# A metaformer block on one core: interleaved channel pairs and small pieces in the scan, and the norm's inverse root as a power on POOL

## The chip, the cores and the metric

The kernel runs on one core of a Trainium2 chip, in fp32 throughout. The metric is the device time of one execution in microseconds (us). PE is TensorE (matmul), DVE is VectorE, ACT is ScalarE, POOL is GpSimd, and SP is SyncE, which issues nearly all of the kernel's DMAs.

## The reference, cut to what matters

The input is 8 samples of 384 channels and 32 x 32 positions. Each sample is read as L = 1024 tokens of C = 384 channels. The layer adds a state-space ("mamba") branch with an MLP, then a feed-forward branch with sign-binarised weights and activations that are quantised by sample:

```python
t = (t - mu) * rsqrt(var + 1e-05) * ln_w + ln_b       # after a norm over channels, eps 1e-6
xm, z = split(t @ in_proj_w.T)                        # 768 channels each
xc = silu(conv3(xm) + conv_b)                         # causal, three taps
dt, Bm, Cm = split(xc @ x_proj_w.T, [24, 24 + 16])
dt = softplus(dt @ dt_proj_w.T + dt_proj_b)
dA = exp(dt[..., None] * -exp(A_log));  dBu = (dt * xc)[..., None] * Bm[:, :, None, :]
h = dA_t * h + dBu_t;  y_t = sum_n(h * C_t)           # a scan over 1024 tokens, 16 states
y = (y + xc * D) * silu(z)
x = x + gelu((y @ out_proj_w.T) @ mlp_w1.T + b1) @ mlp_w2.T + b2
t = t + ffn(norm(t))     # two "bitlinear" layers with gelu between; samples 0 to 4 only
```

The bitlinear layers quantise in five groups along the batch of 8, so that a group is one sample and the samples 5 to 7 get zero from the feed-forward branch.

## The kernel before, in words

**Who sets the order.** The kernel first writes down all operations as a list (`write_down`, `Plan.add`), each with an engine, a planner's cost in us, what it reads and writes (whole tiles or parts of them), and a priority, called lane. `Plan.run` then goes through a planned time, picks for each engine what can start, and emits the instructions in that order. Each engine runs its own instructions strictly in that order on the chip; the plan's times play no part any more. Lane 0 is the scan, 1 and 4 the front of the coming samples (`s1` and its norms), 2 the back (`s3`), 5 and 6 the feed-forward part, 7 the binarising of weights, and -1 the scan's sums on PE. On DVE and POOL the planner prefers ready work of lanes above 0. Small evictions of PSUM and affine steps (`affine`) may go to ACT or to DVE (or POOL), whichever is free. Costs come from formulas such as `c_act`, `c_dve` and `c_pool`. Where PE would idle in the plan for over 0.7 us, a `spare` matmul (L412) is put in that has no use but to occupy PE. Tiles come from rings of a fixed number of buffers (`self.rings`); an operation that needs a new buffer waits until one is free. PSUM has three buffers for matmul results (`mm`), one for the scan's sums (`y`), and two of double size for `da`.

**The front, `s1`.** For each sample and each half of 512 tokens: `norm` (L543) makes the mean by matmuls with ones (`p_sum`), spreads it over the partitions by a matmul (`p_mean`, L567), subtracts on DVE (L578), squares on ACT, sums again (`p_var`), takes Sqrt on ACT on 128x128 (with a table load where the table was another), the reciprocal on DVE (L590), spreads this (`p_r`), and multiplies on DVE (L592). Then come `p_in` and the convolution (L661), Silu over all six channel blocks at once (one 128x3072 instruction), `p_dbc` (the x_proj), `p_bc` (which adds the two halves of B and C, L703), six `p_dt` matmuls (L722) with 24 useful rows each, Softplus over 128x3072, six products dt * xc on POOL (L732), the stores of xc, z, dt and dtx to DRAM as whole tiles of 128x3072, and `p_z` with Silu.

**The scan, `s2`, `scan`, `scan_tile`.** A unit is 64 channels with 16 states over 1024 tokens (in samples 0 and 7: 128 channels over 512), so 12 units a sample. It is handled in tiles of 128 partitions = 32 channels x 4 states: two tiles for each of four quads of states, eight in a unit. For each tile: ACT makes exp(dt * A) into `da` (L510), POOL multiplies `u = dtx_r * B` (L886), DVE scans (L890; the result goes to `u` or `da`), and the product with C is made on POOL (L904) or DVE (L907), as `on_pool` says by quad and unit. PE adds the four states and folds into `py` with four matmuls of 32 columns side by side (L842), for two quads together. `dt_r` and `dtx_r` are copies of rows from DRAM, each repeated on four partitions.

**The back, `s3` and `ffn`.** `s3` has `p_out` (36 matmuls a sample), `p_h` and `p_o` (72 each) with Gelu on half of the hidden channels at once (128x3072). `ffn` has two `p_y` layers for samples 0 to 4, clipping on POOL (L1088) and Gelu on 128x3072. `binarise` sums the weights' columns by matmuls with ones (L1018), once.

Of the kernel before, what the change touches and what calls it, by code (L numbers as in the profile page):

```python
# [33 lines left out]
P = 128  # L34
B, C, L = 8, 384, 1024
KC = C // P
DI = 768
# [5 lines left out]
HK = KH // 2  # L43
T = 512
# [49 lines left out]

def c_pool(n):
    return 0.18 + n * 0.00214
# [33 lines left out]
class Piece:  # L130
# [8 lines left out]

    def __getitem__(self, part):  # L140
        return self, part

# [209 lines left out]
class Layer:  # L352
    def __init__(self, ctx, tc, a, out):
# [9 lines left out]
        def ring(tag, bufs, where=sbuf):  # L363
# [7 lines left out]
            "front": ring("front", 2), "t_f": ring("t_f", 2), "w_f": ring("w_f", 3),  # L371
            "dbc": ring("dbc", 1), "halo": ring("halo", 2),

            "dt_r": ring("dt_r", 3), "dtx_r": ring("dtx_r", 3), "u": ring("u", 9),
# [4 lines left out]
            "yg": ring("yg", 1), "hid": ring("hid", 2), "t_b": ring("t_b", 1), "w_b": ring("w_b", 3),  # L379
            "w6": ring("w6", 2), "w6_n": ring("w6_n", 2), "res": ring("res", 2),  # L380

            "t_n": ring("t_n", 2), "small": ring("small", 7),

            "mm": ring("mm", 3, psum), "sq": ring("sq", 1),
            "rstd": ring("rstd", 2),
# [6 lines left out]
        for b in range(B):  # L392
            for name in ("dt", "dtx"):
                self.dram[name, b] = handed(f"{name}_d{b}", [DI, L])
# [24 lines left out]

    def constants(self):
        nc, a, const = self.nc, self.a, self.const
        small = const.tile([P, 3], F32, name="small")
        one, self.eps_m, self.eps_f = (small[:, i : i + 1] for i in range(3))
        for at, value in ((one, 1.0), (self.eps_m, E1 * E2), (self.eps_f, E_FFN)):
            nc.vector.memset(at, value)
# [8 lines left out]
        self.pick = const.tile([P, 2 * NS], F32, name="pick")  # L436
        nc.vector.tensor_add(self.pick, ident[:, DQ : 2 * DQ], ident[:, DP + DQ : DP + 2 * DQ])
        self.edge = const.tile([P, KD, 2], F32, name="edge")
# [50 lines left out]
    def matmuls(self, p, w, t, k0, n, start, stop, r, claim, w0=0):  # L489


        def emit():
            for k in range(n):
                self.nc.tensor.matmul(  # L494
                    p.real, w.real[:, w0 + k, :], t.real[:, k0 + k, :],
                    start=start and k == 0, stop=stop and k == n - 1,
                )
# [45 lines left out]
    def norm(self, t, eps, scale):  # L543
# [17 lines left out]
        def spread(src, name):  # L561
            p = self.piece("mm", [P, T], name)

            def emit():
                for g in range(G):
                    one = self.ident[:, g * DQ : g * DQ + 1].to_broadcast([P, P])
                    nc.tensor.matmul(  # L567
                        p.real[:, g * TG : (g + 1) * TG], one, src.real, start=True, stop=True
# [16 lines left out]
        rstd = self.piece("rstd", [P, TG], "rstd")  # L585
        self.act(
            lambda: rstd.real, lambda: p_var.real, AF.Sqrt, c_act(TG), r=[p_var], w=[rstd],
# [684 lines left out]
```

## Time and profile before

| | |
|---|---|
| three runs | 3261.88 us median (3261.76 to 3268.25) |
| the profiled execution, device time | 3262.23 us |
| its span, first to last instruction | 3260.4 us, granted TensorE clock 0.984 |
| ACT table loads | 222 x 1283 ns, 284.8 us |
| exp into `da`, 128x1024 | 576 x 1116 ns, 639.4 us |
| scans on DVE, 128x1024 | 312 x 2285 ns and 264 x 2278 ns |
| `p_h`, `p_o` matmuls on PE | 513.6 and 506.7 us |
| DMA | 748.73 MB, mean 230 GB/s, 68.5% of 16 engines |

One matmul of 128x512 in fp32 is two records on PE, of 592 ns each and overlapping. A row of a group gives line, engine, operation, output and inputs, shape, count, then busy time, mean ns of one, and the idle time of the engine just before with what ended most of it. Busy time is the union of the records, so that it can be less than count times mean. "L494" and "L510" are helpers that emit most matmuls and activations; there the tile's name tells them apart.

### The profile page before, as it was taken

What the parts mean: (1) busy time and instruction counts of PE and PEld (TensorE: products, weight loads), DVE (VectorE), ACT (ScalarE), POOL (GpSimd) and SP (SyncE); (2) the same over time, 40 slices, a digit from 0 to 9 for tenths busy, and PEclk for the clock granted to TensorE, in tenths of its full rate; (3) what the DMA queues carried; (4) which work ended last, traced back from release to release, by engine and by line L of the source; (5) the groups of instructions that cost most, each with busy time, mean ns of one, the idle gap of its engine ahead of it and who ended that gap; (6) DMA issues with size and microseconds to landing.
All of it is one profiled execution on the core that took longest, in us unless ns stands there. A gap on an engine that the chain in (4) does not pass through costs nothing.

```text
span 3260.4 us, 34027 instructions
## 1 busy us (share of the span) xinstructions
PE 3122.5 (96%) x11098; PEld 1317.7 (40%) x11098; DVE 2742.3 (84%) x2127; ACT 2024.3 (62%) x2246; POOL 2848.7 (87%) x1371
## 2 busy tenths in 40 slices
PE   8988999999999999999899999999999999999999
PEld 4333433444433434334334344343443534433334
DVE  4778899799978899888998878999788988789880
ACT  4778787656665576665656566755666565656551
POOL 1688899979999989999989999989999899999970
PEclk9998999999999999999999999999999999999999
DMA  6988778657796568675686667866677656766542
GB/s 218 305 282 276 249 250 294 221 183 234 259 322 197 184 230 291 229 238 197 208 298 211 237 211 246 295 225 226 220 275 250 207 185 205 249 187 207 167 141 76
DMA packets 367345, 748.73 MB, mean 230 GB/s; under 512 B 33856, under 2 KB 111168, under 8 KB 367168
## 3 DMA queue, kind: packets, MB, share of 16 engines
q1 hardware_dynamic: 366736, 746.46, 68.5%
q8 instruction: 89, 1.46, 0.2%
q14 instruction: 88, 0.72, 0.1%
q10 hardware_dynamic: 432, 0.09, 0.0%
HBM read 566.06 MB, written 180.36 MB: 229 GB/s over the span
## 4 chain that ended last, share of the span: by engine, by line
PE 74%; DMA 9%; DVE 6%; ACT 5%; issue 2%; POOL 2%; SPq 1%; ACTq 0%; DVEq 0%; POOLq 0%
PE p_y L494 17%; PE p_o L494 14%; PE p_h L494 13%; PE py L842 9%; PE p_out L494 6%; PE p_z L494 6%; PE p_in L494 5%; DVE da L890 2%; DMA w<-in_out_proj_w 2%; DMA w_f<-in_in_proj_w 2%; DVE u L890 1%; ACT L510 1%; DMA w_b<-in_mlp_w 1%; ACT da L510 1%; PE spare L412 1%
## 5 line engine op out<-in xcount | busy, mean ns | idle before, releaser
L886 POOL TENSOR_TENSOR u<-dtx_r,bc 128x1024 f32<-128x1024 f32 x768 | 1790.4, 2362 | 72.3 <-DMA dtx_r<-dtx_d 46.3
L510 ACT ACTIVATE da<-dt_r,a_neg 128x1024 f32<-128x1024 f32 (+1 forms) x960 | 902.7, 945 | 534.0 <-DVE u L907 331.1
L904 POOL TENSOR_TENSOR u<-u,bc 128x1024 f32<-128x1024 f32 x352 | 828.4, 2364 | 121.5 <-DVE u L890 115.5
L890 DVE TENSOR_TENSOR_SCAN da<-da,u 128x1024 f32<-128x1024 f32 (+1 forms) x416 | 840.5, 2020 | 111.6 <-POOL u L886 62.9
L890 DVE TENSOR_TENSOR_SCAN u<-da,u 128x1024 f32<-128x1024 f32 (+1 forms) x352 | 699.5, 2010 | 90.3 <-ACT da L510 63.0
L494 PE MATMUL p_h<-t,w_b 128*128 128x512 f32 x1152 | 513.6, 600 | 10.9 <-DMA w_b<-in_mlp_w 9.9
L907 DVE TENSOR_TENSOR u<-da,bc 128x1024 f32<-128x1024 f32 x416 | 507.9, 1221 | 10.5 <-ACT state L901 0.3
L494 PE MATMUL p_o<-g,w 128*128 128x512 f32 x1152 | 506.7, 595 | 5.4 <-ACT g L510 2.9
L842 PE MATMUL py<-u,fold 128*32 128x512 f32 x3072 | 376.6, 605 | 4.5 <-DVE u L907 4.5
L494 PEld LDWEIGHTS p_h<-t,w_b 128*128 128x128 f32 x1152 | 214.7, 190 | 298.1 <-issue 256.4
L494 PEld LDWEIGHTS p_o<-g,w 128*128 128x128 f32 x1152 | 215.9, 190 | 292.0 <-issue 277.3
L494 PE MATMUL p_y<-tn,w_b 128*128 128x512 f32 x720 | 324.9, 598 | 4.0 <-DVE tn L592 3.3
L494 PE MATMUL p_y<-gf,w_n 128*128 128x512 f32 x720 | 319.0, 599 | 6.7 <-DMA w_n<-bin_w 4.0
L510 ACT ACT_TABLE_LOAD x222 | 284.8, 1283 | 11.7 <-DVE xc L661 7.3
L494 PE MATMUL p_out<-yg,w 128*128 128x512 f32 x552 | 249.2, 604 | 8.9 <-DMA w<-in_out_proj_w 4.3
L494 PE MATMUL p_z<-t,w_f 128*128 128x512 f32 x504 | 232.5, 611 | 8.2 <-DMA w_f<-in_in_proj_w 6.2
L494 PE MATMUL p_in<-t,w_f 128*128 128x512 f32 x504 | 228.3, 602 | 10.8 <-DMA w_f<-in_in_proj_w 8.6
L494 PEld LDWEIGHTS p_y<-gf,w_n 128*128 128x128 f32 x720 | 135.1, 191 | 187.6 <-issue 172.4
L494 PEld LDWEIGHTS p_y<-tn,w_b 128*128 128x128 f32 x720 | 133.9, 190 | 183.9 <-issue 155.4
L842 PEld LDWEIGHTS py<-u,fold 128*32 128x32 f32 x3072 | 81.5, 110 | 261.1 <-issue 203.2
L525 ACT ACTIVATE g<-p_h,v_vecs 128x512 f32<-128x512 f32 x157 | 106.3, 681 | 120.9 <-PE p_h L494 120.7
L525 ACT ACTIVATE y<-p_y,v_vecs 128x512 f32<-128x512 f32 x138 | 94.1, 683 | 130.0 <-PE p_y L494 100.3
(112 smaller groups left out, 2700.3 us busy)
## 6 DMA issues: line engine op xcount, KB each, us to landing
dtx_r<-dtx_d SPq DMA_DIRECT2D x144, 512.0 KB, 5.8
dt_r<-dt_d SPq DMA_DIRECT2D x144, 512.0 KB, 6.0
w_b<-in_mlp_w SPq DMA_DIRECT2D x192, 192.0 KB, 2.9
w<-in_mlp_w SPq DMA_DIRECT2D x96, 384.0 KB, 3.6
w_f<-in_in_proj_w SPq DMA_DIRECT2D x168, 192.0 KB, 4.2
y_d<-y SPq DMA_DIRECT2D x120, 256.0 KB, 3.4
gf<-y_d SPq DMA_DIRECT2D x20, 1536.0 KB, 9.5
xc_d<-xc SPq DMA_DIRECT2D x16, 1536.0 KB, 7.3
```

The lines of the kernel that those rows point to most:

```text
L412: self.plan.fill = lambda: self.nc.tensor.matmul(self.plan.spare.real[:, : 2 * P], self.ones, self.one.to_broadcast([P, 2 * P]), start=Tru ...
L494: self.nc.tensor.matmul(p.real, w.real[:, w0 + k, :], t.real[:, k0 + k, :], start=start and k == 0, stop=stop and k == n - 1,)
L510: lambda: self.nc.scalar.activation(out(), in_(), func, **{k: v() if callable(v) else v for k, v in kw.items()}),
L525: nc.scalar.activation(out(), in_(), AF.Identity, bias=bias, scale=scale)
L842: nc.tensor.matmul(py.real[p0 : p0 + DQ, :], self.fold, hc, start=False, stop=(q == NQUAD - 1), skip_group_check=True,)
L886: add("POOL", 2.36, lambda: nc.gpsimd.tensor_mul(u.real, dtx_r.real, spread(bq)), r=[dtx_r, bq], w=[u])
L890: add("DVE", (0.2 if half else 0.15) + n * 0.00209, lambda k=k, col=col: nc.vector.tensor_tensor_scan(to.real[:, k, :], da.real[:, k, :], ...
L904: add("POOL", 2.36, lambda: nc.gpsimd.tensor_mul(u.real, u.real, spread(cq)), r=[cq], w=[u])
L907: add("DVE", 1.21, lambda: nc.vector.tensor_mul(u.real, da.real, spread(cq)), r=[da, cq], w=[u])
```

## The change

It has several parts at once.

1. **Interleaved pairs.** dt * xc is stored with two channel blocks' values side by side: `[.., n, 2]`. `scan_tile` becomes `scan_pair`, which handles two tiles: one POOL product over 128x2048 (two of 128x1024 in samples 0 and 7) with the B or C row repeated for each pair of neighbours, two scans and, on DVE, two products that read or write every second element. The product of the last quad is made in place in `dtx_r`. `on_pool` puts the second products of quads 0 and 2, and of quad 1 in every fourth unit, on POOL.
2. **Rings.** `u` has 3 buffers (of double size) in place of 9, `dtx_r` 2 (double) in place of 3.
3. **Small pieces.** Tiles of 128x3072 (`xc`, `z`, `dt`, `yg`, `g`, `gf`) become three or six pieces of 128x1024 with buffers of their own; activations, clips, loads and stores go piece by piece. `mlp_out` issues its matmuls by two.
4. **The norm.** The variance is scaled and evicted (ACT or DVE), turned by a matmul so that it stands in four columns, gets eps added on DVE, and is raised to -0.5 on POOL over 128x4. Sqrt and the reciprocal go.
5. **dt_proj and the rows.** One matmul (`p_all`) adds the halves for dt, B and C and lays dt's low part on two groups of 32 rows; two dt matmuls of 32 rows each then go as a pair. The B and C rows are stored by one DMA instead of four.
6. **Binarising.** The column sums use 32 columns of PE for each of three or four blocks, and the group sums are made by DVE reductions and one more matmul.

The diff's core (layouts of the weights on the host follow the new order of channels and are left out):

```diff
+def c_pair(n):
+    return 0.19 + n * 0.00188
...
-            "front": ring("front", 2), "t_f": ring("t_f", 2), "w_f": ring("w_f", 3),
+            "front": ring("front", 7), "t_f": ring("t_f", 2), "w_f": ring("w_f", 3),
...
-            "dt_r": ring("dt_r", 3), "dtx_r": ring("dtx_r", 3), "u": ring("u", 9),
+            "dt_r": ring("dt_r", 3), "dtx_r": ring("dtx_r", 2), "u": ring("u", 3),
...
-            "yg": ring("yg", 1), "hid": ring("hid", 2), ... "res": ring("res", 2),
+            "yg": ring("yg", 3), "hid": ring("hid", 6), ... "res": ring("res", 4),
...
-        rstd = self.piece("rstd", [P, TG], "rstd")
-        self.act(
-            lambda: rstd.real, lambda: p_var.real, AF.Sqrt, c_act(TG), r=[p_var], w=[rstd],
-            table="sqrt", bias=eps, scale=scale,
-        )
-        add("DVE", 0.93, lambda: nc.vector.reciprocal(rstd.real, rstd.real), w=[rstd])
-        p_r = spread(rstd, "p_r")
+        var = self.piece("rstd", [P, TG], "var")
+        self.affine(lambda: var.real, lambda: p_var.real, [p_var], [var], scale=scale, n=TG)
+        p_turned = self.piece("mm", [P, G], "p_turned")
+        add("PE", 0.5, lambda: nc.tensor.matmul(
+            p_turned.real, var.real, self.ident[:, ::DQ], start=True, stop=True
+        ), r=[var], w=[p_turned])
+        rstd = self.piece("root", [P, G], "rstd")
+        add("DVE", 0.1, lambda: nc.vector.tensor_scalar_add(rstd.real, p_turned.real, eps),
+            r=[p_turned], w=[rstd])
+        add("POOL", 0.8, lambda: nc.gpsimd.tensor_tensor(
+            rstd.real, rstd.real, self.power.to_broadcast([P, G]), ALU.pow
+        ), w=[rstd])
+        p_r = spread(rstd, "p_r", True)
...
+                def two(k=k, pds=pds, dbc=dbc, ws=ws):
+                    for i in range(2):
+                        rows = slice(i * DQ, (i + 1) * DQ)
+                        nc.tensor.matmul(
+                            pds[i].real, ws[i].real[rows, (k + i) % KC, :], dbc.real[rows, :],
+                            start=True, stop=True,
+                        )
...
+                add("POOL", 2.35, lambda p=p, dtx=dtx, xc=xc, dt=dt: nc.gpsimd.tensor_mul(
+                    dtx.real.rearrange("p n i -> p i n"), xc.pieces[p].real, dt.pieces[p].real
+                ), r=[xc[2 * p], xc[2 * p + 1], dt[2 * p], dt[2 * p + 1]], w=[dtx])
...
-        return q == 0 or (q == 2 and (i == 0 or m % 3))
+        return q % 2 == 0 or (q == 1 and m % 4 == 0)
...
+        def product(t, x, row):
+            nc.gpsimd.tensor_mul(
+                u.real[:, x], t.real[:, x], row.real.unsqueeze(2).to_broadcast([P, n, 2])
             )
...
+        for x in range(wide):
+            add("POOL", c_pair(2 * n), lambda x=x: product(dtxs, x, bq), r=[dtxs[x], bq],
+                w=parts[x])
+        for t, mine in enumerate(cols):
+            da = self.piece("da", [P, wide, n], "da")
+            dt_r = dts[t]
...
+            def in_u(i, t=t):
+                return u.real[:, 0, :, t] if wide == 1 else u.real[:, t, :, i]
...
+                        nc.vector.tensor_mul(u.real[:, 0, :, t], da.real[:, 0, :], cq.real)
...
+        if on_pool:
+            for x in range(wide):
+                add("POOL", c_pair(2 * n), lambda x=x: product(u, x, cq), r=[cq], w=parts[x])
```

The sums then read every second element, `u.real[:, 0, h, i]`, where `u` is viewed as `[P, wide, n, 2]` with the halves of the tokens as `h`:

```diff
-                        for p0, hc in parts:
+                        parts = [u.real[:, 0, h, i] for i in both for h in HALVES] if (
+                            half is None) else [u.real[:, x, :, i] for i in both for x in both]
+                        for g, hc in enumerate(parts):
                             nc.tensor.matmul(
-                                py.real[p0 : p0 + DQ, :], self.fold, hc,
+                                py.real[g * DQ : (g + 1) * DQ, :], self.fold, hc,
```

## The prediction, as put on record

> **What bounds the kernel now.** I read the page's busy shares first, then the same shares over three stretches (up to the first scan product on POOL at 105 us, from there to the last scan sum on PE at 3178 us, and the tail), then the groups and who waits for whom.
>
> ```profile
> PE 3122.5 (96%) x11098; PEld 1317.7 (40%) x11098; DVE 2742.3 (84%) x2127; ACT 2024.3 (62%) x2246; POOL 2848.7 (87%) x1371
> ```
> ```profile
> 0.00:105.00 105.00, 90.77 (x444) 46.50 (x446) 43.04 (x61) 51.89 (x63) 12.67 (x18) 0.97 0.74 245
> 105.00:3178.00 3073.00, 2953.28 (x10470) 1236.72 (x10472) 2695.59 (x2062) 1956.25 (x2166) 2836.08 (x1353) 0.98 0.70 233
> 3178.00:3260.00 82.00, 78.50 (x190) 34.49 (x182) 3.70 (x5) 16.12 (x17) 0.00 (x0) 1.00 0.25 77
> ```
> ```profile
> L886 POOL TENSOR_TENSOR u<-dtx_r,bc 128x1024 f32<-128x1024 f32 x768 | 1790.4, 2362 | 72.3 <-DMA dtx_r<-dtx_d 46.3
> L904 POOL TENSOR_TENSOR u<-u,bc 128x1024 f32<-128x1024 f32 x352 | 828.4, 2364 | 121.5 <-DVE u L890 115.5
> L907 DVE TENSOR_TENSOR u<-da,bc 128x1024 f32<-128x1024 f32 x416 | 507.9, 1221 | 10.5 <-ACT state L901 0.3
> L842 PE MATMUL py<-u,fold 128*32 128x512 f32 x3072 | 376.6, 605 | 4.5 <-DVE u L907 4.5
> ```
> ```profile
> L722 PE MATMUL p_dt<-dbc,w_f 128*128 128x512 f32 x168 | 81.9, 620 | 9.5 <-ACT dt L525 6.0 <-ACT rows L523 3.4
> L722 PE MATMUL p_dt<-dbc,w_b 128*128 128x512 f32 x24 | 11.4, 608 | 0.9 <-DVE xc L661 0.9
> L412 PE MATMUL spare<-small 128*128 128x256 f32 x314 | 80.0, 396 | 0.1
> L590 DVE RECIPROCAL rstd<-rstd 128x128 f32<-128x128 f32 x26 | 24.2, 937 | 1.8 <-ACT rstd L510 1.3
> ```
> ```profile
> PE p_r L567 <- DVE rstd L590: 10.5, 6, 3.7
> ```
>
> The reader is to see that no engine bounds it alone. (The rows of the second fence give, for each stretch, its length, then busy us and count of PE, PEld, DVE, ACT and POOL, then clock, DMA share and GB/s; the groups give count, busy us, mean ns of one, and the idle time before them with its cause.) In the scan stretch of 3073 us PE is busy 2953 (96%), but about 71 of that is the `spare` filler, which the planner puts only where PE would have nothing: useful PE work is 2882, so PE lacks work for 191 us. POOL is busy 92%, DVE 88%. The 96 units (8 samples, 12 each) take 32.0 us each; of these PE needs 30.0, POOL 29.5, DVE 28.1. Three nearly equal loads that hand work to each other lose 2 us per unit in waiting: POOL waits 115.5 us for DVE's scans, and PE runs into filler. A saving on one engine pays only if the others leave room. The tail is PE alone.
>
> [...] The interleaved tiles are read every 8 bytes[...]; no row of before shows such a stride. [...] four `py` matmuls take 376.6/384 = 0.98 us.
>
> **The change, part by part.** Counts after the change are from the order of the built programs.
>
> *POOL products.* Removed: 1790.4 + 828.4 us. Added: 450 of 2048 elements and 304 of 1024 (754 where there were 1120, though DVE's share of the second products falls from 416/768 to 332/768). The new shape, one operand repeated for each two neighbours, is in no row of before, so its price is bounded. Above: nothing is gained, two of today's less one fixed part,[...] 4.50 us. Below: one-input rows on POOL take 0.93 ns per element (2898 ns at 3072, 1474 at 1536), two-input ones 2.12 (2362 at 1024, 1275 at 512); if the repeated operand is read half as often, half of the difference goes, 1.53 ns, 3.3 us. The middle is 3.9. I take 4.04 (2.12 at 1024): near the middle, and the value that the diff's c_pair gives the planner, whose c_pool, c_act and c_dve lie within 1.1% of the rows that the trace does show (2.371 against 2.362, 1.110 against 1.116, 1.234 against 1.221). An estimate, then. 450 x 4.04 + 304 x 2.12 = 2462 against 2619: -157. At 4.50 (2.36): +124; at 3.3 (1.75): -602.
> *Other POOL.* `dtx` 48 x 2.36 = 113 for 118.6; clipping in 60 pieces of 1.0 (from 2.898 at 3072 and 1.474 at 1536 elements) 60 for 57.9; edge and state copies 104 x 0.2 = 21 for 15; the power of 4 elements 26 x 0.8 = 21 (0.2 as the smallest POOL rows, to 2: 5 to 52). Together +23. POOL: -134, to about 2715; at 4.50 +147; at 3.3 -579.
> *DVE.* 84 fewer products x 1.221 = -103; 26 reciprocals -24; 26 additions x 0.155 = +4; binarising's reductions replace others of about their size. -123. Strided scans I take at today's 2.28[...]; 0 to +100 if not.
> *ACT.* 48 fewer table loads x 1.283 = -62, Sqrt -9 and +6 for its affine, 300 pieces x 1.116 instead of 278 = +57, wider copies +4: about -4. At 62% this is off the path: if its cover went, a whole 57 us would show.
> *PE.* p_dt: 96 matmuls, 93.3 us, become 48 pairs. Side by side 0.97 each (46.6), else 93; I take 1.07: -42. p_all 16 x 0.97 instead of p_bc's 6.7: +9. p_turned 26 x 0.3 = +8. The binarising sums, 18.7, in six sets at `py`'s 0.98: -13. Net -38 (to +4 without overlap).
> *Waits.* The norm's root now goes PE, DVE, POOL, PE. Behind POOL's queue it waits for up to one product, half of one on average (2.0); 0.27 + 0.3 + 0.16 + 0.8 + 2.0 = 3.5 us where Sqrt and reciprocal took 1.3 (2.6 with a table load). Queued behind p_r on PE is everything, since PE keeps its order; in the order after, p_r sometimes follows p_turned with only one or two small groups between. 1 to 2.2 us x 26 = 26 to 57; PE work covers most, I count 10 (0 to 50). POOL's pow also holds back at most 0.8 us of products.
> *DMAs.* SP issues 2091 before and 2255 after, at about half a us each (525 ns for `dtx_r`): 82 us more on a queue with much room; bytes of `dtx_r` are the same. Stores and loads in pieces can start earlier: small gain, counted at nothing (it is covered by PE's other work; if not, the 46.3 us that POOL waits for `dtx_r` can return, since that ring now has two buffers for one per unit).
> *Rings.* Three `u` of double size, and the last product in place of `dtx_r`: a unit's buffers come free at its two sums. With POOL leading by one pair that suffices; counted at nothing, at worst the 21.6 us POOL now waits for `py` doubles.
>
> **The sum.** Against the profiled execution (span 3260.4, device time 3262.2; the runs' median is 3261.9, so no shift). Upper case, *waiting stays*: only PE's work shrinks and the norm's wait comes on top, 3262 - 38 + 10 = 3234. Lower case, *POOL keeps its share*: (2836 - 134)/0.923 = 2927, + 105 + 82 + 2 = 3116 (the 2 is device time over span); PE's 2844 useful us in it would be 97%, which is possible, as the best slices of today reach 99%. Room on POOL and DVE is now 5 to 10% below PE's need in place of 2 to 6%, so part of the waiting must go; I have no row that gives the part and take the middle: (3234 + 3116)/2 = 3175. At 3.3 us POOL would leave PE alone as the bound: its 2844 at the 99% of its best slices is 2873, + 187 + 2 + 10 = 3072 with nothing else in the way; I put the low end at 3095, since PE's stalls on DMA and norms stay. Next late is PE's own work, then the chain scan to product to sum.
>
> **Rivals.**
> 1. *Waiting stays* because pairs double the grain: a second product waits for two scans (4.6 us). For it: the 115.5 us wait on DVE. Against: DVE gets freer too. 3234, faster still.
> 2. *The product isn't cheaper* (slower): place L886/L904's successor, price 4.50. POOL then has 2836 + 147 = 2983 in the stretch; at a share of 95% (between today's 92 and the 97 of its fullest stretches) 3140 + 189 = 3329. It decides where POOL's total is back at today's: 4.04 + 0.46 x 134/281 = 4.26 us.[...] Against: the planner's record.
> 3. *PE reads interleaved sums slowly* (slower): at double, 384 x 0.86 = +330: 3500. It decides from (3262 - 3175)/384 = 0.23 us per set.[...]
> 4. *No measurable change*: coarser waits and norm stalls eat some 90 us: 3262.
>
> **How the numbers follow.** Forecast (3095 to 3210) 0.60; rival 1 (3210 to 3255) 0.15; rival 4 within 0.2% (about what a measurement of this kernel can tell from no change) 0.05; rival 2 0.14; rival 3 and the like 0.06. Faster 0.75, same 0.05, slower 0.20. The range, 3095 to 3290, takes the forecast, rivals 1 and 4 and rival 2's milder part. The forecast's own range is 3095 to 3210.
>
> **What would show it.** The 2048-element POOL row near 4.04; POOL near 2715 and DVE near 2620 busy; p_dt under 55 us; `py` still near 377; spare filler and PE's idle time both smaller; table loads 174; p_r's wait on POOL under 25. A product above 4.26, `py` rows above 0.7 us or PE waiting long for rstd would make it wrong.

## The result, and the profile after

The changed kernel takes 3309.31 us (median of 4 runs, 3296.7 to 3317.63) against 3264.64 us for the kernel before in the same series: ratio 1.0127, 95% interval 1.0105 to 1.015. It is slower by 1.3%, where 3175 us was forecast. The profiled execution took 3317.63 us with a span of 3315.7 us and a granted clock of 0.974; before it was 3260.4 us and 0.984. So the profile explains a difference of 55 us, some ten more than the medians.

The busy shares of the page after, and the same three stretches as before (up to the first scan product on POOL, now at 95 us; up to the last scan sum, now at 3243 us; the tail):

```profile
PE 3129.7 (94%) x10964; PEld 1290.3 (39%) x10964; DVE 2643.6 (80%) x2080; ACT 1979.2 (60%) x2362; POOL 2749.3 (83%) x1050
```
```profile
0.00:95.00 95.00, 83.56 (x446) 41.84 (x446) 39.22 (x72) 47.52 (x59) 12.87 (x19) 1.00 0.70 229
95.00:3243.00 3148.00, 2977.04 (x10359) 1218.03 (x10358) 2600.88 (x2004) 1915.29 (x2283) 2736.39 (x1031) 0.97 0.70 230
3243.00:3316.00 73.00, 69.06 (x162) 30.40 (x160) 3.53 (x5) 16.38 (x21) 0.00 (x0) 1.00 0.26 78
```

The reader is to see that POOL and DVE each got about 99 us less to do (2848.7 and 2742.3 before), and that the scan stretch became 75 us longer all the same: POOL fills 87% of it, where it filled 92%. PE's busy time did not fall. The groups of the scan and of the parts that PE was to save:

```profile
L924 POOL TENSOR_TENSOR u<-dtx_r,bc 128x2048 f32<-128x2048 f32 x216 | 881.6, 4093 | 162.3 <-PE py L889 111.0 <-issue 45.9 <-POOL dtx_r L924 3.3
L924 POOL TENSOR_TENSOR u<-u,bc 128x2048 f32<-128x2048 f32 x162 | 662.2, 4091 | 62.3 <-DVE u L949 62.3
L924 POOL TENSOR_TENSOR u<-dtx_r,bc 128x1024 f32<-128x1024 f32 x144 | 304.7, 2137 | 18.7 <-PE py L889 11.3 <-DMA dtx_r<-dtx_d 3.9 <-DVE u L949 1.9
L889 PE MATMUL py<-u,fold 128*32 128x512 f32 x2304 | 308.0, 630 | 0.2 <-POOL u L924 0.2
L889 PE MATMUL py<-dtx_r,fold 128*32 128x512 f32 x768 | 106.7, 616 | 0.4 <-DVE dtx_r L971 0.4
L765 PE MATMUL p_dt<-dbc,w_f 32*128 32x512 f32 x168 | 51.6, 657 | 5.1 <-ACT dt L553 2.7 <-DVE rstd L624 2.3
L433 PE MATMUL spare<-small 128*128 128x256 f32 x220 | 58.5, 405 | 2.3 <-DVE t L610 0.9 <-ACT y L553 0.7 <-ACT dt L553 0.4
```
```profile
PE p_z L522 <- DMA w_f<-in_in_proj_w: 42.0, 14, 5.1
...
PE p_in L522 <- DMA w_f<-in_in_proj_w: 8.4, 4, 4.5
...
PE p_r L598 <- POOL rstd L626: 3.4, 4, 1.1
```
```profile
POOL dtx L780 <- DMA dtx_d<-dtx: 63.0, 19, 6.5
...
POOL rstd L626 <- DVE rstd L624: 30.2, 10, 15.1
```

Three waits of the kernel before, to compare them with:

```profile
POOL u L886 <- PE py L842: 21.6, 11, 5.3
...
PE p_in L494 <- DMA w_f<-in_in_proj_w: 8.6, 6, 6.4
...
PE p_z L494 <- DMA w_f<-in_in_proj_w: 6.2, 4, 2.7
```

The product's price is as forecast (4.09 us for 2048 elements, two of 2.36 before). But the first products wait 122 us in all (111.0 and 11.3) for buffers that PE's sums have yet to release, where that was 21.6, and PE waits 50 us for the weights of `p_z` and `p_in` (`w_f`), where that was 15. Two waits on POOL are new: `dtx` waits 63.0 us for the store of the `dtx` before it, and the norm's power 30.2 us for DVE.

PE falls behind early. The first 500 us of the kernel before, and then of the changed one (columns as above):

```profile
0.00:500.00 500.00, 451.74 (x1794) 196.74 (x1794) 387.85 (x393) 363.74 (x476) 361.23 (x223) 0.97 0.80 261
```
```profile
0.00:500.00 500.00, 419.41 (x1673) 175.32 (x1674) 359.49 (x390) 335.26 (x471) 348.09 (x228) 0.92 0.76 251
```

PE is busy 32 us less there, and what it does runs slower. The same matmuls of the same shape, in the first 500 us of before and of after:

```profile
L494 PE MATMUL p_z<-t,w_f 128*128 128x512 f32 x180 | 81.8, 609 | 4.6 <-DMA w_f<-in_in_proj_w 2.6 <-DVE xc L661 1.9
L494 PE MATMUL p_in<-t,w_f 128*128 128x512 f32 x180 | 80.4, 601 | 2.3 <-ACT da L510 1.7 <-DMA w_f<-in_in_proj_w 0.6
```
```profile
L522 PE MATMUL p_in<-t,w_f 128*128 128x512 f32 x180 | 91.8, 663 | 19.9 <-DMA w_f<-in_in_proj_w 7.2 <-ACT dt L553 6.7 <-DVE xc L703 2.8
L522 PE MATMUL p_z<-t,w_f 128*128 128x512 f32 x144 | 74.0, 666 | 21.6 <-DMA w_f<-in_in_proj_w 20.1 <-DVE mean L1128 1.4
```

180 `p_in` records take 663 ns each instead of 601, and the idle time ahead of them is 19.9 us instead of 2.3. Idle time and a low clock lie together: PE is busy 419 of the 500 us at a mean clock of 0.92, and 452 of them at 0.97 before. That a gap also lowers the clock, and so is paid twice, is not shown by these records.

But this early gap alone does not decide the time. The scan is hardly behind at that point: the sums of the first sample's twelve units end at 561 us instead of 551. The lag then grows through the rest of the kernel, to 28 us after the fourth sample and 64 after the last (3243 us instead of 3179). And a run below, c_is_b_wf5, is 29 us faster than its control, c_is_b, though its first 500 us are no fuller.

One account puts the runs below side by side (before_norm, before_plus and after_whole are versions between the two kernels, described under "The parts"). A span is made of PE's useful busy time (busy less filler) and of the rest (idle and filler). The first I split by the mean granted clock: busy less filler, times the clock, is the work at full clock, and what is left is what the clock costs. The split is an estimate from these numbers: the mean clock is taken for the whole span, PE's time is taken to go as one over the clock, which no run shows by itself, and one step of 0.001 in the clock is 3 us.

| kernel | PE busy | filler | clock | work at full clock | cost of the clock | idle and filler | span |
|---|---|---|---|---|---|---|---|
| before | 3122.5 | 80.0 | 0.984 | 2993.8 | 48.7 | 217.9 | 3260.4 |
| before_norm | 3127.5 | 93.4 | 0.990 | 3003.8 | 30.3 | 221.4 | 3255.5 |
| before_plus | 3135.2 | 91.7 | 0.977 | 2973.5 | 70.0 | 238.7 | 3282.2 |
| after_whole | 3176.5 | 115.2 | 0.975 | 2984.8 | 76.5 | 311.2 | 3372.5 |
| after | 3129.7 | 58.5 | 0.974 | 2991.3 | 79.9 | 244.5 | 3315.7 |

From before to after: work -2.5, clock +31.2, idle and filler +26.6, together +55.3.

### The profile page after: what moved, and what is told of

It reads as the page before. It is cut to its first block, busy times and chain, and to the rows that moved or that the text cites. A ratio compares the mean times of both kernels' runs of the same rounds, so it can differ in the third digit from the quotient of the medians.

```text
span 3315.7 us, 33789 instructions
## 1 busy us (share of the span) xinstructions
PE 3129.7 (94%) x10964; PEld 1290.3 (39%) x10964; DVE 2643.6 (80%) x2080; ACT 1979.2 (60%) x2362; POOL 2749.3 (83%) x1050
## 4 chain that ended last, share of the span: by engine, by line
PE 70%; DMA 14%; DVE 5%; ACT 4%; POOL 3%; issue 2%; SPq 1%; POOLq 0%; DVEq 0%; ACTq 0%
PE p_y L522 16%; PE p_o L522 13%; PE p_h L522 12%; PE py L889 9%; PE p_out L522 7%; PE p_in L522 5%; PE p_z L522 4%; DMA w_f<-in_in_proj_w 3%; POOL u L924 2%; DVE da L949 2%; DMA dtx_d<-dtx 1%; DVE u L949 1%; DMA w_n<-bin_w 1%; DMA yg_d<-zr 1%; DMA w_b<-in_mlp_w 1%
## 5 line engine op out<-in xcount | busy, mean ns | idle before, releaser
L924 POOL TENSOR_TENSOR u<-dtx_r,bc 128x2048 f32<-128x2048 f32 (+1 forms) x360 | 1186.3, 3311 | 181.0 <-PE py L889 122.3
L924 POOL TENSOR_TENSOR u<-u,bc 128x2048 f32<-128x2048 f32 (+1 forms) x274 | 901.5, 3294 | 112.9 <-DVE u L949 106.6
L949 DVE TENSOR_TENSOR_SCAN u<-da,u 128x1024 f32<-128x1024 f32 (+1 forms) x436 | 868.6, 2007 | 117.4 <-POOL u L924 77.7
L949 DVE TENSOR_TENSOR_SCAN da<-da,dtx_r 128x1024 f32<-128x1024 f32 (+1 forms) x192 | 388.2, 2022 | 98.7 <-POOL dtx_r L924 60.3
L924 POOL TENSOR_TENSOR dtx_r<-dtx_r,bc 128x2048 f32<-128x2048 f32 (+1 forms) x120 | 396.8, 3313 | 1.4
L889 PE MATMUL py<-u,fold 128*32 128x512 f32 x2304 | 308.0, 630 | 0.2 <-POOL u L924 0.2
L949 DVE TENSOR_TENSOR_SCAN da<-da,u 128x1024 f32<-128x1024 f32 (+1 forms) x140 | 286.2, 2044 | 27.2 <-POOL u L924 13.7
L522 PE MATMUL p_z<-t,w_f 128*128 128x512 f32 x504 | 244.6, 635 | 45.0 <-DMA w_f<-in_in_proj_w 42.0
L522 PE MATMUL p_in<-t,w_f 128*128 128x512 f32 x504 | 239.1, 624 | 23.9 <-DMA w_f<-in_in_proj_w 8.4
L522 PE MATMUL p_out<-yg,w 128*128 128x512 f32 x552 | 250.8, 606 | 11.3 <-DMA yg<-yg_d 4.6
L538 ACT ACT_TABLE_LOAD x174 | 223.2, 1283 | 3.1
L780 POOL TENSOR_TENSOR dtx<-xc,dt 128x1024 f32<-128x1024 f32 x48 | 114.2, 2379 | 106.2 <-DMA dtx_d<-dtx 63.0
```

What stands on the lines that cost most here:

```text
L522: self.nc.tensor.matmul(p.real, w.real[:, w0 + k, :], t.at(k0 + k), start=start and k == 0, stop=stop and k == n - 1,)
L538: lambda: self.nc.scalar.activation(out(), in_(), func, **{k: v() if callable(v) else v for k, v in kw.items()}),
L780: add("POOL", 2.35, lambda p=p, dtx=dtx, xc=xc, dt=dt: nc.gpsimd.tensor_mul(dtx.real.rearrange("p n i -> p i n"), xc.pieces[p].real, dt.pi ...
L889: nc.tensor.matmul(py.real[g * DQ : (g + 1) * DQ, :], self.fold, hc, start=False, stop=(q == NQUAD - 1), skip_group_check=True,)
L924: nc.gpsimd.tensor_mul(u.real[:, x], t.real[:, x], row.real.unsqueeze(2).to_broadcast([P, n, 2]))
L949: da=da, in_u=in_u: nc.vector.tensor_tensor_scan(to(i), da.real[:, i, :], in_u(i), state.real[:, col : col + 1] if half else 0.0, ALU.mult ...
```

## The experiments

Ratios are against the kernel before on the same chip, with 95% intervals. Some kernels keep the order of instructions that they start from, and differ in one thing. Others are planned anew, so that all of the order moves; two null changes, which alter the order and no operation, tell what that alone can do.

### Null changes: how much is a new order worth?

```diff
-SLACK = 1.4
+SLACK = 1.5
```

> The changed kernel with one constant of the planner changed that has no meaning for the computation (SLACK 1.4 to 1.5): another order of the same instructions. Theory of the rings: within 15 us of 3309. Theory that the order is luck: it differs by 30 us or more.

Measured: 3327.47 us, 1.0194 (1.017 to 1.0218), some 18 us above the changed kernel, for a constant of the planner that changes no operation. That lies between the two expectations.

> The kernel before with the planner's SLACK at 1.5 instead of 1.4, which alters the order and no operation. If orders of the same work differ by the 18 us seen for the changed kernel or more, and the order of before is a good one among them: 3275 to 3310. If before's work gives about the same time in any order: 3255 to 3270.

Measured: 3261.37 us, 0.9983 (0.9973 to 0.9992). This second order of the kernel before is as good as the first, so its time is not the luck of one order. Between kernels planned anew from the changed one, I give no cause to a difference of less than 20 us. Two null changes are few, though: a larger difference can still be the order's.

### Does less POOL work make the kernel before faster?

```diff
-            add("POOL", 2.36, lambda: nc.gpsimd.tensor_mul(u.real, u.real, spread(cq)),
+            add("POOL", 2.36, lambda: nc.gpsimd.tensor_mul(
+                u.real[:, :, n * 11 // 64 :], u.real[:, :, n * 11 // 64 :], spread(cq)[:, :, n * 11 // 64 :]),
```

> The kernel before in its own order, with each second product on POOL leaving out the first 11 of 64 elements of its width (a changed computation), so that POOL has about 135 us less to do, as the change gives it, and nothing else differs. My prediction's lower case (POOL keeps its share): 3120 to 3180. The rival (POOL is not the bound; PE with its own stalls is): 3240 to 3262, with POOL's busy share falling from 87% to 84% and its waits growing by 100 us or more.

Measured: 3259.49 us, 0.9979 (0.9969 to 0.9989). POOL's busy time fell by 125 us and the time by 5.6. The page's busy line and the group of the shortened products:

```profile
PE 3121.5 (96%) x11098; PEld 1318.0 (40%) x11098; DVE 2742.2 (84%) x2127; ACT 2025.2 (62%) x2246; POOL 2723.6 (84%) x1371
```
```profile
L904 POOL TENSOR_TENSOR u<-u,bc 128x848 f32<-128x848 f32 x352 | 699.1, 1989 | 189.7 <-DVE u L890 181.9 <-DMA dtx_r<-dtx_d 1.4 <-PE p_in L494 1.0
```

The wait for DVE's scan ahead of the same products was 115.5 us and is 181.9. All POOL waits of the trace together rose from 314 to 435 us: of the 125 us saved, 121 came back as waiting. This is the run that the prediction needed, and it could have been thought of before: same order, one engine relieved. Two things it does not tell: what relief of DVE is worth, which the change brings as well, and what an order planned for the shorter products would gain.

### Does less PE work make the changed kernel faster?

```diff
             for k in range(n):
+                if p.name == "p_o" and k0 + k in (5, 11):
+                    if k == n - 1 and stop:
+                        continue
+                    continue
...
-                    start=start and k == 0, stop=stop and k == n - 1,
+                    start=start and k == 0,
+                    stop=stop and (k == n - 1 or p.name == "p_o" and k0 + k == 10),
```

> The changed kernel in its own order, with two of the twelve matmuls of each p_o left out (a changed computation), 96 of 576, about 82 us of PE. If PE with its stalls on DMA is the bound: 3309 - 82 x 0.7 to 0.95 = 3230 to 3252. If the chain of pairs through DVE and POOL is the bound: 3285 to 3310, with PE waiting more for the sums' inputs.

Measured: 3284.16 us, 1.0064 (1.0042 to 1.0086). The group of `p_o` in the changed kernel, then here:

```profile
L522 PE MATMUL p_o<-g,w 128*128 128x512 f32 x1152 | 511.8, 597 | 3.0 <-DMA w<-in_mlp_w 3.0
```
```profile
L526 PE MATMUL p_o<-g,w 128*128 128x512 f32 x960 | 434.0, 601 | 22.7 <-DMA w<-in_mlp_w 21.4 <-DVE res L1043 0.7 <-ACT g L543 0.6
```

`p_o` fell by 78 us and the time by 25, to the edge of what the second theory allows. This saving on PE pays about a third; idle and filler rose from 244.5 to 280.5 us, and some half of that is `p_o` itself, which now waits for its own weights (21.4 us instead of 3.0).

### What do the filler and the clock do?

```diff
-            self.plan.spare.real[:, : 2 * P], self.ones,
-            self.one.to_broadcast([P, 2 * P]), start=True, stop=True,
+            self.plan.spare.real[:, :16], self.ones,
+            self.one.to_broadcast([P, 16]), start=True, stop=True,
```

> The kernel before in its own order, each filler matmul cut from 256 columns to 16, so that PE stands idle where it was filled (80 us of filler become some 15). Clock theory: with the filler gone the granted clock falls from 0.984 to 0.965 to 0.978 and useful matmuls take longer, 3275 to 3305. Rival, that the clock is only a sign of idle time and costs nothing: 3255 to 3268, clock lower or not.

Measured: 3268.08 us, 1.0009 (0.9995 to 1.0024), at a clock of 0.972 to 0.976 in its twelve runs. Filler fell from 80.0 to 47.5 us, less than I expected.

The same lines of the changed kernel with `4 * P`:

> The changed kernel in its own order, each filler matmul widened from 256 to 512 columns, so that the filler takes about 110 us of PE instead of 58. Clock theory: the clock rises from 0.974 to 0.98 or more and the time falls by 5 to 20 us, to 3289 to 3304, if the filler lies where PE is idle anyway. Rival, that the filler only stands in the way: 3310 to 3340.

Measured: 3333.96 us, 1.0198 (1.0173 to 1.0223), clock 0.979; filler rose from 58.5 to 106.5 us, the time by 25. Both forecasts of the clock theory failed, but these runs do not free the clock of blame. By the account above, in the profiled executions, the first has 12 us less of idle and filler and 31 us more of clock (its profiled execution, 3280.6 us, is among the two slowest of the twelve); the second has 29 us more of idle and filler and 16 us less of clock. So the clock moved with the filler in both, by 0.010 and 0.005, and the two terms work against each other. What the runs show is that the filler is worth nothing on balance and costs time when widened, so that it does not lie only where PE would be idle.

### Do the shorter binarising sums starve PE?

```diff
-                        pm.real[g * DQ : (g + 1) * DQ, :], self.ones[:, :DQ],
-                        w.real[:, k - ks.start, :], start=(k < lanes), stop=(k >= kt - lanes),
+                        pm.real, self.ones,
+                        w.real[:, k - ks.start, :], start=(k == 0), stop=(k == kt - 1),
...
-            nc.vector.tensor_scalar_mul(mean.real, mean.real, -1.0 / (gs * kt * P * DQ))
+            nc.vector.tensor_scalar_mul(mean.real, mean.real, -1.0 / (gs * kt * P * DQ * lanes))
```

> The changed kernel in its own order, with binarising's column sums on all 128 columns again, one after the other (six sets of seven become 21 whole matmuls, about 12 us more of PE in the first 500 us); the whole computation is kept. Theory that the shorter sums left PE with too little to do and so lowered the clock: 3285 to 3302, with the clock loss of the first 500 us (29 us) falling by 8 or more. Rival: 3309 to 3322, the same or longer by its own work.

Measured: 3321.88 us, 1.0167 (1.0145 to 1.019). `p_sums` went from 6.4 to 21.2 us and the time rose by 13, just about its own work (the intervals overlap). The theory fell.

### Do the sums pay for reading every second element?

```diff
-                        parts = [u.real[:, 0, h, i] for i in both for h in HALVES] if (
-                            half is None) else [u.real[:, x, :, i] for i in both for x in both]
+                        flat = u.real.rearrange("p x n i -> p (x n i)")
+                        parts = [flat[:, g * T : (g + 1) * T] for g in range(G)]
```

> The changed kernel with the same order, but the sums on PE read the interleaved tiles as contiguous runs of 512 (so they add up the wrong elements; the amount of work is the same). Theory of the longer sums: py's record falls from 612 to 592 ns, its busy time from 415 towards 380, and the time falls by 20 to 40 us. Theory of the rings: the record falls likewise, the time by 0 to 15.

Measured: 3301.58 us, 1.0112 (1.0089 to 1.0135). The rows of `py` in this run:

```profile
L889 PE MATMUL py<-u,fold 128*32 128x512 f32 x2304 | 293.0, 608 | 2.0 <-POOL u L924 1.3 <-POOL w L1145 0.7
L889 PE MATMUL py<-dtx_r,fold 128*32 128x512 f32 x768 | 103.5, 601 | 0.0
```

Against 630 and 616 ns: the stride costs 2 to 4% of a record, 18 us of busy time in all, and 8 us of time, which lie within the intervals.

### Do the three buffers of `u`, or the one of `dtx`, hold POOL back?

To have room, the control `c_is_b` lets B's rows stand for C's, too. Its order is planned anew.

```diff
-b_q[q], c_q[q] = quad_rows(q), quad_rows(NQUAD + q)
+b_q[q] = c_q[q] = quad_rows(q)
```

> The changed kernel, but the C rows aren't loaded: the B rows are used for both products (the computation is changed in that one part), which frees 16 KB of each partition. It is the control for the next run; its 40 loads fewer are replanned. All theories: 3309 within 0.7%, so 3287 to 3330. If the order that the planner happens to lay decides by itself, it may lie outside.

Measured: 3306.39 us, 1.0127 (1.0106 to 1.0149); as the changed kernel. Then, in the control's order, five real buffers of `u` where the planner counted three:

```diff
-"u": ring("u", 3),
+"u": ring("u", 3, real=5),
```

> As the control, with exactly its order of instructions on every engine, but five real buffers for u instead of three (B rows again used for C). Theory of the rings (POOL waits 122 us for the sums on PE because it can run only three tiles ahead): POOL's wait for py falls under 40 us, and the time falls by 40 us or more against the control. Theory of the longer sums on PE, and that of PE as the bound anyway: the wait on POOL goes, but the time stays within 10 us.

Measured: 3304.35 us, 1.0129 (1.0104 to 1.0154). The products' rows in the control, then in this run:

```profile
L924 POOL TENSOR_TENSOR u<-dtx_r,bc 128x2048 f32<-128x2048 f32 x216 | 880.8, 4089 | 157.4 <-PE py L889 83.4 <-issue 57.4 <-DMA bc<-rows_d 8.8
L924 POOL TENSOR_TENSOR u<-u,bc 128x2048 f32<-128x2048 f32 x162 | 661.6, 4087 | 68.8 <-DVE u L949 65.2 <-PE p_dbc L734 1.9 <-DMA xr<-xc_d 1.8
```
```profile
L924 POOL TENSOR_TENSOR u<-dtx_r,bc 128x2048 f32<-128x2048 f32 x216 | 880.0, 4091 | 8.7 <-DMA bc<-rows_d 4.5 <-PE p_y L522 4.3
L924 POOL TENSOR_TENSOR u<-u,bc 128x2048 f32<-128x2048 f32 x162 | 661.7, 4086 | 188.2 <-DVE u L949 174.3 <-DMA bc<-rows_d 11.0 <-DMA xr<-xc_d 2.8
```

The wait for PE's sums is gone (83.4 us in the control), and the wait for DVE's scans has grown from 65.2 to 174.3. In this order the ring was where the wait showed, not what set the pace; an order that is planned for five buffers was not run. With two buffers of its own for `dtx`, on top of the control:

```diff
-            "mm": ring("mm", 3, psum), "sq": ring("sq", 1),
+            "mm": ring("mm", 3, psum), "sq": ring("sq", 1), "dtx": ring("dtx", 2),
...
-                dtx = self.piece("sq", [P, T, 2], "dtx")
+                dtx = self.piece("dtx", [P, T, 2], "dtx")
```

> The same control with a ring of its own (two buffers) for the interleaved product dtx, which in the change takes turns with the norm's squares in one buffer. Theory of the dtx buffer: POOL's waits for the store of dtx (63 us) and for p_var (32 us) go, PE is busy over 440 us in the first 500, and the time falls to about 3280. Theory of the weights or of the norm: the waits go, but the time stays within 10 us of 3306.

Measured: 3329.07 us, 1.019 (1.0154 to 1.0226): not faster, in a new order. POOL's wait for the store of `dtx` fell from 48.9 us in the control to 22.6 and the one for `p_var` went, but PE is busy 419.57 us in the first 500, no more than before. The theory has no support.

### Is it the weights?

On the control, `w_f` with five buffers:

```diff
-"w_f": ring("w_f", 3),
+"w_f": ring("w_f", 5),
```

> The changed kernel with the B rows used for C as well (as in the control, 3306), and five buffers instead of three for the front's weights w_f. The runs so far show that PE falls back in the first 500 us (busy 416 to 425 us, before 452) and never makes it up. Theory that the paired dt matmuls, which hold two of three weight buffers across a pair, starve the front: PE's waits for w_f (50 us in the change) fall under 20, PE is busy over 440 in the first 500 us, and the time falls to about 3280. Theory of the dtx buffer: no more than 10 us from the control.

Measured: 3277.51 us, 1.0038 (1.0028 to 1.0048), and PE's waits for `w_f` fell to 2.6 us. PE's first 500 us did not fill, however. The control, then this run:

```profile
0.00:500.00 500.00, 424.87 (x1712) 180.61 (x1713) 362.26 (x394) 340.85 (x481) 344.19 (x224) 0.94 0.75 247
```
```profile
0.00:500.00 500.00, 424.03 (x1687) 177.57 (x1688) 365.89 (x392) 333.58 (x479) 343.56 (x224) 0.92 0.76 249
```

I took the weights for the cause all the same. Two runs with the whole computation then spoke against it. One drops the third load of dt_proj's weights in each half, which the change had brought in:

```diff
-                if k % KC != 2:
+                if k == 0:
                     w = self.weights(r_w, KC, a["dt_proj_w"][k // KC])
-                else:
+                elif k % KC == 2:
                     w, before = self.weights(r_w, KC, a["dt_proj_w"][1]), w
```

> The changed kernel with dt_proj's weights loaded twice per half instead of three times (the third pair uses the tile already there); the whole computation is kept, and the order is planned anew. Weights theory: the waits of PE for w_f, 50 us after the change, fall under 20, as in the run with five buffers, and the time falls by 15 to 35 us to 3275 to 3295 (planner noise of about 18 us either way counted in). Rival, that the third load is harmless and only the number of buffers matters: no change beyond that noise, 3300 to 3320, with w_f waits still at 40 or more.

Measured: 3311.13 us, 1.0136 (1.0109 to 1.0164), with 45.6 us of waits for `w_f`. The other has five buffers for `w_f` and two for `res`:

> The changed kernel with five buffers for w_f instead of three, paid for with res (two instead of four); the whole computation is kept, the order is planned anew. Weights theory: PE's waits for w_f under 15 us and 3265 to 3295, as with B used for C. Rival, that the gain there was the planner's luck: 3300 to 3330.

Measured: 3312.52 us, 1.0137 (1.0115 to 1.0159), with 2.0 us of waits for `w_f`. PE's longest waits there:

```profile
PE p_h L522 <- DMA w_b<-in_mlp_w: 17.9, 11, 3.5
PE p_in L522 <- DMA w_b<-in_in_proj_w: 15.7, 2, 9.1
PE p_var L580 <- ACT sq L538: 8.9, 6, 3.6
```

The wait was taken away and others took its place: all of PE's waits in the trace are 167 us, 181 in the changed kernel and 133 before. The weights theory found no support in the whole computation; one doubt remains, since this run also has two buffers of `res` fewer, and no run separates what they do. That the control with five buffers was 29 us faster I can't put down to the buffers. If it is the order's, then a new order can do more than the 18 us of the null change.

### The parts, added one after the other

The versions before_norm, before_plus, after_whole and the changed kernel lie on one ladder, each with more of the change than the one ahead of it. All are planned anew.

The norm alone, in the kernel before, and the reverse in the control (the lines of the change's fourth part):

> The kernel before with the change's norm alone (root as a power on POOL). Theory of the norm's longer chain: slower by 20 us or more. The others: within 10 us of 3265, at best 10 to 20 us faster, since 50 table loads and 26 reciprocals go.

Measured: 3251.83 us, 0.996 (0.9948 to 0.9972). This version beats both kernels, by 13 us against the kernel before. That is more than the 6 us of that kernel's null change and less than the 18 of the other, so that the norm may or may not be the reason.

> The same control with the norm of before (Sqrt on ACT and the reciprocal on DVE over 128x128) put back. Theory of the norm's longer chain: PE busy over 440 us in the first 500 us and about 3280. Theory of the dtx buffer or the weights: within 10 us of 3306, or slower by the table loads that come back (some 50 of 1.28 us, on ACT with room).

Measured: 3308.57 us, 1.0137 (1.0109 to 1.0165), 2 us from the control. There the choice of the norm makes no difference that can be told.

Then, on top of the norm, everything that does not touch the scan or the pieces (`small` with four buffers for room; the diff is that of the change, with the weights loaded as in after_reuse):

> The kernel before, with the parts of the change that do not touch the scan or the pieces: the norm's power on POOL, the binarising sums on 32 columns, one matmul that adds the halves of the low rows, and dt's matmuls in pairs with the weights loaded twice. The theory that these parts are sound and that pairs, small pieces and the third weight load cost the time: PE's useful work falls by about 40 us against before, and the time is 3200 to 3250, below the 3252 of the new norm alone. Rival, that a saving on PE is not turned into time because the units' chain through DVE and POOL sets the pace: 3245 to 3265, with PE's filler and idle time larger by what was saved.

Measured: 3290.41 us, 1.0075 (1.0049 to 1.0102): slower than the norm alone by 38 us (1.0075 to 0.996), which neither theory foresaw.

Last, the whole change but the small pieces:

```diff
-PER = 2
+PER = 6
...
-            "front": ring("front", 7), ...
+            "front": ring("front", 2), ...
-            "yg": ring("yg", 3), "hid": ring("hid", 6), ...
+            "yg": ring("yg", 1), "hid": ring("hid", 2), ...
```

> The changed kernel with xc, z, dt, yg, g and gf as whole tiles of 128x3072 again (front 2, yg 1 and hid 2 buffers, one activation, store or load each), everything else of the change kept, the whole computation too; planned anew. Theory that the small pieces cost the time: 3255 to 3280, with the waits of PE for DMA near those of before. Theory that the coarser pairs cost it: 3300 to 3340.

Measured: 3388.17 us, 1.0365 (1.0328 to 1.0402), above both ranges. So the small pieces don't cost, they save 79 us (with the numbers of buffers that go with them); and between before_plus and after_whole, which differ by the pairs and what comes with them (the rings of `u`, `dtx_r` and `res`, `dtx` through `sq`, the share of DVE, the third load), lie 98 us. Who waited in the scan shows in DVE's waits for POOL's products. before_plus first, then after_whole:

```profile
DVE da L907 <- POOL u L903: 61.1, 29, 6.1
DVE u L907 <- POOL u L903: 53.3, 10, 13.4
```
```profile
DVE u L956 <- POOL u L931: 117.2, 58, 6.4
...
DVE da L956 <- POOL dtx_r L931: 99.8, 20, 21.6
```

And the filler that the planner put in, in the same two kernels:

```profile
L412 PE MATMUL spare<-small 128*128 128x256 f32 x346 | 91.7, 406 | 0.4 <-DVE rstd L600 0.2
```
```profile
L433 PE MATMUL spare<-small 128*128 128x256 f32 x448 | 115.2, 400 | 5.0 <-ACT dt L553 3.0 <-DVE q L1179 0.7 <-ACT g L553 0.5
```

DVE waits 217 us for the two kinds of product instead of 114 (and 11.7 us for a third, `da` from `u`), and PE's idle and filler go from 238.7 to 311.2 us. By the account above most of this step is idle time and filler (+72.5 of +90.3 us in the profiled executions). The pieces take that back (-66.7). In the step from before_norm to before_plus, by contrast, the largest term is the clock (+39.7). (The profiled execution of after_whole, 3374 us, lies below its median.)

## Why the prediction was wrong, step by step

- **Part of the waiting must go; take the middle.** This is the step that failed first. The sum went from 3234 to 3175 because POOL and DVE would have more room. before_pool_less gives the part for which I had no row: 125 us of POOL are worth 5.6 us. POOL did not keep its share either, 92% became 87%. With this step at its measured size the forecast would have been about 3228 us: still faster, still wrong. That is 53 of the 134 us between 3175 and 3309; the other 81 lie in the terms below. What relief of DVE is worth was not measured.
- **PE: net -38.** The parts went as forecast: `p_dt` 58.5 us for 93.3 (-35; forecast -42), `p_all` 19.4 for 6.7 (+13; forecast +9), `p_turned` 8.9, `p_sums` with `p_means` 7.2 for 18.7 (-12; forecast -13), some -25 in all. Missing from the sum were the stride of `py` (18 us of busy time) and the clock. before_plus shows it without the scan: by the account above, against the norm alone, work at full clock fell by 30 us, the clock took 40, and idle and filler 17. I had valued PE's matmuls at one price per record, and that price moved: in the first 500 us the same `p_in` took 601 ns in one kernel, at a clock of 0.97, and 663 in the other, at 0.92. That two `p_dt` matmuls in different row groups overlap was my estimate, too: the rows of before show it for the column groups of `py` only. The sum also took PE's saving one for one; after_pe_less got 25 us of time for 78 of work.
- **Rings, counted at nothing.** POOL's wait for `py` was to double at worst, from 21.6; it became 122.3. But five buffers of `u` gained nothing in the control's order: the wait was mis-sized, and taking it away did not give the time back. That `dtx` takes turns with the norm's squares in one buffer had no term at all; POOL's 63.0 us ahead of `dtx` are that.
- **Pairs at the price of their work alone.** The pairs were costed as products at 4.04 us, and their coarser hand-over at nothing in the forecast. With what comes with them they cost 98 us on the ladder, the largest term of all. Rival 4 had "coarser waits and norm stalls eat some 90 us": the norm stalls did not come, and how much of the 98 us the coarser waits are is open.
- **DMAs in pieces, counted at nothing, small gain.** The right sign and far too small: 79 us of gain, once the pairs are there.
- **The norm's wait, 10 us.** `p_r` waits 3.4 us for POOL (10.5 for DVE before). The norm alone came out 13 us faster. Too dear by my count, and PE did not queue up behind POOL as I feared. The other side I had too cheap: the power was to hold back POOL by 0.8 us at most, and POOL stood still for 30.2 us in all ahead of it.
- **POOL -134, DVE -123, ACT about -4.** Measured -99, -99 and -45. The product was priced nearly rightly, 4.09 for 4.04, but 754 of them make that 2484.6 us for 2462. Clipping in pieces took 1202 ns for the 1.0 us that I worked out from longer rows (71.0 us for 60); the two rows came from different clips, one with its bounds read from a tile and one with fixed bounds, and should not have been joined by one line. The power took 1017 ns for 0.8. Scans stayed at 2284 ns, and ACT's table loads became 174, as forecast; ACT's pieces took 1046 ns, where I had put in the 1116 of exp.
- **Rival 2, 3329 us**, lies near the result for a reason that did not hold: its product would have had to cost over 4.26 us, and it took 4.09. For a product that gains nothing the plain rows of before (2362 ns for 1024 elements, 1275 for 512) give 4.54 on a line, an estimate; the 4.50 is within 1% of it. **Rival 3** had the right place, the sums' stride, and the wrong size: it was to decide from 0.23 us per set; 18 us over 384 sets are 0.05. No row of before has such a stride, so the low weight that I gave it was an estimate. Its "double" was reckoned with 0.86 us, the planner's figure for a matmul, though a set took 0.98.
- **Spare filler and idle time both smaller.** Filler fell, 80.0 to 58.5; with idle it rose by 26.6.

What is shown: in the unchanged order of the kernel before, relief of POOL is not time; the pairs with what comes with them cost and small pieces give back. Five buffers for `u` (in the order for three) or `w_f`, one weight load fewer, the norm of before and longer binarising sums each did not bring the time back. What stays open: which part of the pairs costs the 98 us (that it is the grain, a scan that waits for a product of 4.1 us in place of 2.4, is argued from DVE's waits and not isolated), which of before_plus's parts costs the 38 us, or whether its order does, and how far the lower clock of the first 500 us is cause or only company of PE's gaps. The last two steps of the ladder are larger than what a new order did in the null changes (18 us and 6), and than the 29 us of c_is_b_wf5 that found no cause; but each was planned anew, and the 38 us of before_plus are not far above these.

## What to carry to other kernels

When several engines are nearly equally busy, their work need not be a budget to share out: shorten one engine's operations in the unchanged order first, and see whether the time follows; here 125 us gave 5.6. Price a coarser hand-over for the wait that it can make at both ends, not only for the work it saves; cutting the tiles that nothing else needs whole went the other way, by 79 us. And where a planner sets the order, run a change that means nothing before you believe 20 us, and believe no single kernel that a buffer "fixed" until it is so in a second setting: the 29 us of `w_f` did not come back in the next.

## What the runs showed of the hardware

- POOL multiplies by an operand that is repeated for each two neighbours faster than by a plain one: 4093 ns for 2048 elements and 2137 to 2141 for 1024, against 2362 for a plain 1024. One product of 2048 lies 13% below two plain ones of 1024 (4724 ns), one of 1024 about 9% below a plain one.
- PE reads fp32 at every second element almost as fast as contiguous fp32, 630 and 616 ns (the changed kernel) for 608 and 601 (packed_sums): 2 to 4% more for a record.
- Two `p_dt` matmuls of 32 rows each in different row groups took 58.5/48 = 1.22 us together, where two whole ones took 2 x 0.97 (93.3/96): somewhat over a third saved, not half.
- A power on POOL over 4 elements per partition takes 1017 ns, and 26 reciprocals of 937 ns, 26 Sqrt of 367 ns and 48 table loads of 1283 ns went for it.
